# Softmax with one exponential per head, the maximum as bias and the sum accumulated

## The chip, the cores and the metric

One core of a Trainium2 chip. The metric is the device time of one execution in microseconds (us), lower is better. The engines are TensorE (PE; its weight loads are shown apart as PEld), VectorE (DVE), ScalarE (ACT), GpSimd (POOL) and SyncE (SP), which here issues the DMA transfers. Each engine works through a queue of its own in order; they wait for one another by semaphores.

## What is computed

Four graph layers over 128 graphs of 64 nodes with 512 features, all in float32, each with a residual and a layer normalization: a hypergraph convolution, a layer whose weights are exp(tanh) of pair sums, three graph convolutions, and attention with 8 heads of 64 features. The change is in the softmax of the last layer. Cut to what matters:

```python
qkv = (x @ W_qkv).reshape(B, N, HEADS, 3, DIM_HEAD)
q, k, v = (jnp.transpose(qkv[..., i, :], (0, 2, 1, 3)) for i in range(3))
dots = jnp.einsum('bhid,bhjd->bhij', q, k) * scale
dots = jnp.where(m2, dots, -big)
attn = jax.nn.softmax(dots, axis=-1) * LA
attn = attn + LG * adj + LD * jnp.exp(-dist)
out = jnp.einsum('bhij,bhjd->bhid', attn, v)
...
x = _layernorm(x + (out @ W_out + b_out), axis=-1)
```

## The kernel before

The 128 graphs are worked on in 16 groups (NGRP) of 8 graphs, that is 4 pairs of 128 rows. Every group goes through a first half (layers 0 and 1, `first_half`, L753) and a second half (layers 2 and 3, `second_half`, L1079). Three groups are in flight: while group q is in its softmax and output (called t in the list), group q + 1 is in the second half (b), and group q + 2 in the first half (a). The order is written out by hand as lists of step names (L1440 and on): `t.v1 a.c1 t.v b.gt t.soft a.w1a1 a.w1a t.soft2 ... t.ptp`. Inside such an order a scheduler places the instructions on each engine, except where `strict` or `behind` holds them.

All large products go through `multiply` (L546), a scheme with seven products of half size for eight: B11, T1, T2, B21, T3, B22, T4, each of four matmuls, on two or three PSUM banks. Between the products partial results have to be read out of a bank before the next product may add to it:

- after B11 into bank a: `u1`, a copy (L555); T2 adds into bank a afterwards
- after T1 into bank c: `u5` (L555); B22 adds into it later
- after T2 into bank a: `u2` (L555); T3 adds into bank a afterwards
- after T3 into bank a: the addition `dst(1, 1) = pa + s5` (L589); T4 adds into bank a afterwards
- at the end two more additions (L568 for B21, L598 for B22) and a copy of T4's bank (L608)

For the product v of the softmax's own group the copies L555 and L608 are ScalarE's, and the additions L568, L589 and L598 are VectorE's. For the product l0w (the first layer of group q + 2) the read-outs L555 are VectorE's, since a bias is added with them.

The operands of these products are prepared by `graph_T` (L470): matmuls into `gt_l` in PSUM, copied by ScalarE (L492) into `aT_l`, from which VectorE makes the sums `s_l` (`sums`, L518 to L521). The rectifications of l0w's result `h` are ScalarE's (L783).

The softmax of a group works on four tiles (two duos of pairs, two halves h2 of the heads) of 128 rows by 8 heads by 64 columns. `scores` (L1345) takes the products out of PSUM with scale and mask (L1367). `softmax_steps` (L1330) does for each tile: the maximum per head (L1334, VectorE), the subtraction (L1336, VectorE), one exponential over all 512 columns (L1337, ScalarE), the sum per head (L1340, VectorE), its reciprocal (L1341) and the product with it (L1342). The first two tiles are done beside v, the third at `t.soft`, the fourth at `t.soft2`; then `turn_probs` (L1382) turns the tiles on TensorE (`ptp`). ScalarE keeps one table of functions at a time; the first exponential of a group stands behind a table load.

Of the kernel before, what the change touches and what calls it, by code (L numbers as in the profile page):

```python
# [10 lines left out]
AF = mybir.ActivationFunctionType  # L11
ALU = mybir.AluOpType
AX = mybir.AxisListType
# [28 lines left out]
def kernel(  # L42
# [31 lines left out]
    NGRP = NPAIR // G  # L74
# [56 lines left out]
    ten, vec, act = Engine(nc.tensor, PE), Engine(nc.vector, DVE), Engine(nc.scalar, ACT)  # L131
# [305 lines left out]
    def bcast(t, n):  # L437

        return t.unsqueeze(2).to_broadcast([P, n, C])
# [806 lines left out]
    def last_rows(g, probs, v, left):  # L1246
# [4 lines left out]
        next(gen)  # L1251
        yield "v1"
        steps = [[softmax_steps(g, duo, probs[duo], h2) for h2 in range(2)] for duo in range(2)]
        for n in range(2):
            for h2 in range(2):
# [74 lines left out]
    def softmax_steps(g, duo, ds, h2):  # L1330

        d, key = ds[h2], f"{g['q']}_{duo}_{h2}"
        mx = small.tile([P, 8], FP, name=f"mx_{key}", tag="mx")
        vec.reduce_max(mx, d, axis=AX.X)  # L1334
        yield
        vec.tensor_sub(d, d, bcast(mx, 8))  # L1336
        act.activation(d, d, AF.Exp)  # L1337
        yield
        sm = small.tile([P, 8], FP, name=f"sum_{key}", tag="sum")
        vec.reduce_sum(sm, d, axis=AX.X)  # L1340
        vec.reciprocal(sm, sm)  # L1341
        vec.tensor_mul(d, d, bcast(sm, 8))  # L1342
        yield
# [34 lines left out]
    def softmax(g, duo, ds, h2s):  # L1378
        for h2 in h2s:
            whole(softmax_steps(g, duo, ds, h2))  # L1380
# [230 lines left out]
```

## Time and profile before

| what | value |
|---|---|
| time of the runs | 2734.22 us median of 3 (2732.8, 2734.22, 2735.39) |
| profiled execution: its span | 2732.1 us (what lies around the span is not listed apart) |
| TensorE busy | 2714.7 us, 99% |
| weight loads of TensorE busy | 2347.7 us, 86% |
| VectorE busy | 2077.8 us, 76% |
| ScalarE busy | 803.9 us, 29% |
| maximum, subtraction, sum, product of the softmax (L1334, L1336, L1340, L1342) | 676, 686, 681, 690 ns each, 60 of each and 4 more in the last group under another line |
| exponential over 512 columns (L1337) | 628 ns each, 64 |
| table load of ScalarE | 1283 ns each |
| granted clock of TensorE | 1.00 |

How to read it: busy time of an engine is the time in which it executes; a pair "mean 628" beside "x64" is the duration of one instruction from its start to its written result, and instructions that follow each other overlap, so the pitch from start to start is shorter. In the timeline each row has a start, the time that the row covers, the engine, the line of the kernel, the operation with its result and operands, and in brackets how long the engine sat idle before it and whose result ended that. In rows of groups the numbers behind the bar are the busy time in all, the mean of one in ns, and the engine's idle time before them.

### The profile page before, as it was taken

The page shows a single profiled execution, that of the slowest core. Times are in us where ns is not written, and L with a number is a line of the kernel's source. Part 1 is how long each engine was busy: PE and PEld are TensorE (multiplying, and loading weights), DVE is VectorE, ACT ScalarE, POOL GpSimd, SP SyncE. Part 2 cuts the span into 40 slices and gives each one's busy share as a digit, 9 for nine tenths or more (in the row PEclk, how much of TensorE's full clock was granted, in tenths as well). Part 3 has the DMA queues.
Part 4 walks back from the last instruction along what each step waited for, and adds up shares of the span by engine and source line. Part 5 has one row for each costly group of instructions (what it writes and reads, how often), then busy time and mean ns, then how long its engine had stood idle before and what let it go on. Part 6 is the DMA issues. An engine that isn't in the chain of part 4 may idle for free.

```text
span 2732.1 us, 67726 instructions
## 1 busy us (share of the span) xinstructions
PE 2714.7 (99%) x28770; PEld 2347.7 (86%) x28770; DVE 2077.8 (76%) x4111; ACT 803.9 (29%) x1440; POOL 38.0 (1%) x71
## 2 busy tenths in 40 slices
PE   9999999999999999999999999999999999999998
PEld 7888888888888888888888888888888888888887
DVE  6878687876877778777786877778677687776766
ACT  3323223232232332323223233232322323233232
POOL 2000000000000000000000000000000000000000
PEclk9999999999999999999999999999999999999999
DMA  7545454454544545455454554545545455454541
GB/s 257 179 129 154 123 175 140 142 162 131 173 131 139 168 129 170 130 145 168 134 165 129 146 165 133 164 129 151 163 130 167 130 154 157 128 166 129 158 125 63
DMA packets 309532, 405.14 MB, mean 148 GB/s; under 512 B 57424, under 2 KB 185456, under 8 KB 309232
## 3 DMA queue, kind: packets, MB, share of 16 engines
q1 hardware_dynamic: 304256, 385.45, 48.2%
q0 software_dynamic: 4832, 15.24, 1.5%
q8 instruction: 228, 3.74, 0.6%
q14 instruction: 72, 0.59, 0.1%
q10 hardware_dynamic: 144, 0.13, 0.0%
HBM read 369.78 MB, written 30.93 MB: 147 GB/s over the span
## 4 chain that ended last, share of the span: by engine, by line
PE 96%; DVE 3%; ACT 1%; issue 0%; DMA 0%; DVEq 0%
PE a_l0w L539 15%; PE b_l0w L539 7%; PE a_l2b L539 4%; PE a_q L539 4%; PE a_k L539 4%; PE a_l2a L539 4%; PE a_v L539 4%; PE c_l0w L539 4%; PE a_l1w L539 4%; PE a_wo L539 4%; PE a_l2c L539 4%; PE gt_l L481 3%; PE gt_l0h L481 2%; PE b_l2a L539 2%; PE b_l1w L539 2%; PE b_l2b L539 2%
## 5 line engine op out<-in xcount | busy, mean ns | idle before, releaser
L539 PE MATMUL a_l0w<-w2w,aT_l0h 128*128 128x256 f32 x720 | 164.3, 381 | 0.0
L457 DVE BATCH_NORM_STATS2 st_l<-x 128x6 f32<-128x512 f32 x244 | 157.9, 676 | 0.6
L539 PEld LDWEIGHTS a_l0w<-w2w,aT_l0h 128*128 128x128 f32 x720 | 135.6, 190 | 18.8
L463 DVE TENSOR_SCALAR x<-x,mv_l,rs_l 128x512 f32<-128x512 f32 x244 | 119.3, 543 | 2.2
L539 PE MATMUL b_l0w<-w2w,s_l0h 128*128 128x256 f32 x480 | 108.5, 379 | 0.0
L783 ACT ACTIVATE h<-h 128x1024 f32<-128x1024 f32 (+1 forms) x58 | 55.0, 948 | 178.5 <-DVE h L598 157.4
L539 PEld LDWEIGHTS b_l0w<-w2w,s_l0h 128*128 128x128 f32 x480 | 91.1, 190 | 12.5
L1140 ACT ACTIVATE aT_h<-gth,gb_col 128x256 f32<-128x256 f32 x124 | 47.2, 491 | 159.0 <-PE gth L1128 159.0
L447 ACT ACTIVATE rs_l<-mv_l,eps_t 128x4 f32<-128x4 f32 (+1 forms) x63 | 18.8, 298 | 252.3 <-DVE mv_l L458 245.0
L492 ACT COPY aT_l<-gt_l 128x512 f32<-128x512 f32 x148 | 78.1, 597 | 46.4 <-PE gt_l L481 46.4
L555 DVE TENSOR_TENSOR u_l0w<-a_l0w,b_bc 128x512 f32<-128x512 f32 x56 | 38.6, 689 | 69.2 <-PE a_l0w L539 69.2
L539 PE MATMUL a_l2b<-gwbw,aT_h 128*128 128x256 f32 x360 | 86.6, 383 | 0.0
L539 PE MATMUL a_l2c<-gwcw,aT_h 128*128 128x256 f32 x360 | 86.3, 382 | 0.0
L539 PE MATMUL a_q<-aT_xT,wqw 128*128 128x256 f32 x360 | 85.1, 379 | 0.5 <-ACT aT_xT L1194 0.5
L539 PE MATMUL a_l1w<-ww,aT_l 128*128 128x256 f32 x360 | 85.1, 379 | 0.2 <-ACT aT_l L492 0.2
L539 PE MATMUL a_l2a<-aT_l,gwaw 128*128 128x256 f32 x360 | 85.0, 379 | 0.0
L539 PE MATMUL a_k<-aT_xT,wkw 128*128 128x256 f32 x360 | 85.0, 379 | 0.0
L539 PE MATMUL a_v<-wvw,aT_xT 128*128 128x256 f32 x336 | 81.1, 384 | 0.5 <-issue 0.5
L539 PE MATMUL a_l0w<-w1aw,aT_l 128*128 128x256 f32 x336 | 80.8, 383 | 0.0
L539 PE MATMUL a_wo<-wow,aT_oT 128*128 128x256 f32 x336 | 79.5, 379 | 0.0
L539 PE MATMUL a_l0w<-w1bw,aT_l 128*128 128x256 f32 x336 | 79.4, 379 | 0.0
L539 PEld LDWEIGHTS a_l2c<-gwcw,aT_h 128*128 128x128 f32 x360 | 67.2, 190 | 11.6 <-ACT u_l2c L555 3.0
(532 smaller groups left out, 6489.0 us busy)
## 6 DMA issues: line engine op xcount, KB each, us to landing
w2w<-w2k SPq DMA_DIRECT2D x210, 256.0 KB, 2.7
x<-in_x_dram SPq DMA_DIRECT2D x15, 1024.0 KB, 5.8
w1aw<-w1ak SPq DMA_DIRECT2D x60, 256.0 KB, 2.7
w1bw<-w1bk SPq DMA_DIRECT2D x60, 256.0 KB, 2.8
ww<-wk SPq DMA_DIRECT2D x60, 256.0 KB, 2.7
gwaw<-gwak SPq DMA_DIRECT2D x60, 256.0 KB, 3.4
gwbw<-gwbk SPq DMA_DIRECT2D x60, 256.0 KB, 2.7
gwcw<-gwck SPq DMA_DIRECT2D x60, 256.0 KB, 2.7
```

Of the source, the lines that this page charges most:

```text
L447: act.activation(rs[:, at], mv[:, at, 1], AF.Sqrt, bias=eps_t)
L457: vec.bn_stats(st, xg[:, p, :])
L463: vec.tensor_scalar(xg[:, p, :], xg[:, p, :], mv[:, p, 0:1], rs[:, p : p + 1], ALU.subtract, ALU.mult)
L481: ten.matmul(ps[g][f * C : (f + 1) * C, c, p, :], src(2 * duo + p)[rows, c0 : c0 + C], mat[rows, 2 * duo + p, :], start=True, stop=True,)
L492: act.copy(o[:, :, :, g, :], ps[g])
L539: ten.matmul(acc[:, blk, :], lhsT, rhs, start=(first and blk == 0 and i == 0), stop=(last and i == n_k - 1), skip_group_check=True,)
L555: last_add[f"{key}.{what}"] = (act.copy(t, ps) if res is None else vec.tensor_add(t, ps, res(m, n))).ins
L783: act.activation(hn, hn, AF.Relu)
L1140: act.activation(o[:, :, h, :], cols, AF.Relu, bias=gb2_col[:, k : k + 1])
```

## The change

For the groups 1 to 14 (`by_heads`) the maximum is taken with its sign turned, and the exponential is issued once per head: 8 instructions of 64 columns, each with the head's negated maximum as bias column and the sum over the 64 columns as accumulated output. The subtraction and the sum on VectorE fall away there. Groups 0 and 15 keep the old instructions. The points at which the steps can be interrupted (`yield`) stay where they were: behind the maximum, and behind the exponential; they are used for group 15 alone.

```diff
         mx = small.tile([P, 8], FP, name=f"mx_{key}", tag="mx")
-        vec.reduce_max(mx, d, axis=AX.X)
-        yield
-        vec.tensor_sub(d, d, bcast(mx, 8))
-        act.activation(d, d, AF.Exp)
+        by_heads = 0 < g["q"] < NGRP - 1
+        if by_heads:
+            vec.tensor_reduce(mx, d, axis=AX.X, op=ALU.max, negate=True)
+        else:
+            vec.reduce_max(mx, d, axis=AX.X)
         yield
         sm = small.tile([P, 8], FP, name=f"sum_{key}", tag="sum")
-        vec.reduce_sum(sm, d, axis=AX.X)
+        if by_heads:
+            for n in range(8):
+                act.activation(d[:, n], d[:, n], AF.Exp, bias=mx[:, n : n + 1], accum_out=sm[:, n : n + 1])
+        else:
+            vec.tensor_sub(d, d, bcast(mx, 8))
+            act.activation(d, d, AF.Exp)
+        yield
+        if not by_heads:
+            vec.reduce_sum(sm, d, axis=AX.X)
         vec.reciprocal(sm, sm)
         vec.tensor_mul(d, d, bcast(sm, 8))
         yield
```

## The prediction

> **What bounds the kernel now.** I read the page's totals and chain first, then the groups by shape, then one steady stretch of the timeline (908 to 975 us). All times below are from the profiled execution.
>
> ```profile
> PE 2714.7 (99%) x28770; PEld 2347.7 (86%) x28770; DVE 2077.8 (76%) x4111; ACT 803.9 (29%) x1440; POOL 38.0 (1%) x71
> ...
> PE 96%; DVE 3%; ACT 1%; issue 0%; DMA 0%; DVEq 0%
> ```
>
> TensorE works without a gap: 2714.7 of 2732.1 us busy, and it is 96% of the chain that ends last. VectorE time taken away is worth nothing by itself; all that can be had is the 17.4 us in which TensorE isn't busy, 5.3 of them one wait at the start. A delay of TensorE, however, lengthens the run by its whole length. So I ask where ScalarE and VectorE hand something to TensorE with little to spare. The stretch of one softmax:
>
> ```profile
> 915.16 1.27 DVE L1334 TENSOR_REDUCE mx<-sm 128x8 f32<-128x512 f32 x2
> ...
> 916.84 0.59 ACT L555 COPY u_v<-a_v 128x512 f32<-128x512 f32 x1 [3.87 <-PE a_v L539]
> 917.45 1.28 ACT L1337 ACT_TABLE_LOAD   x1
> ...
> 918.10 1.70 PEld L539 LDWEIGHTS a_v<-wvw,s_xT 128*128 128x128 f32 x8
> ...
> 918.74 0.63 ACT L1337 ACTIVATE sm<-sm 128x512 f32<-128x512 f32 x1
> 919.28 0.57 ACT L555 COPY u_v<-b_v 128x512 f32<-128x512 f32 x1
> ...
> 921.35 2.05 ACT L492 COPY aT_l<-gt_l 128x512 f32<-128x512 f32 x4 [0.46 <-PE gt_l L481]
> ...
> 923.43 0.69 DVE L518 TENSOR_TENSOR s_l<-aT_l 128x512 f32<-128x512 f32 x1 [0.82 <-ACT aT_l L492]
> ...
> 925.50 1.70 PEld L539 LDWEIGHTS b_v<-wvw,s_xT 128*128 128x128 f32 x8
> ...
> 926.57 0.68 DVE L589 TENSOR_TENSOR v<-a_v,u_v 128x512 f32<-128x512 f32 x1
> 927.31 1.62 PEld L539 LDWEIGHTS a_v<-wvw,aT_xT 128*128 128x128 f32 x8
> ```
>
> The last two lines matter most. T4, the last product of v, adds into the bank that L589 has to read first. L589 ends at 926.57 + 0.68 = 927.25 and T4's weights start at 927.31. Products come 1.73 apart (916.37, 918.10), so 925.50 + 1.73 = 927.23 was its turn: it has already waited 0.08 us. VectorE has no slack here at all. Similarly T2 (918.10) needs the copy that ended at 917.43, 0.67 us earlier.
>
> **What the change removes and adds.** In 14 of 16 groups (q = 1 to 14) each of four tiles loses a subtraction (0.686) and a sum (0.681) on VectorE: 56 x 1.37 = 77 us of VectorE work, nearly all beside TensorE work, so worth nothing. The maximum keeps its price (negated in the same instruction). On ScalarE one exponential per tile becomes eight; the old one advances the queue by 919.28 - 918.74 = 0.54.
>
> **The price of one head.** Rows of small ScalarE instructions with a column as bias, and VectorE's read of an accumulator:
>
> ```profile
> L1105 ACT ACTIVATE aT_h<-aT_h,gb_col 128x512 f32<-128x512 f32 x56 | 37.4, 715 | 74.2 <-DVE aT_h L598 73.7
> ...
> L447 ACT ACTIVATE rs_h<-mvh,eps_t 128x2 f32<-128x2 f32 x30 | 7.2, 288 | 0.2
> ```
>
> ```profile
> L829 DVE DVE_READ_ACCUMULATOR xwa<-x,wa_bc 128x1 f32 x60 | 5.1, 85 | 0.0
> ```
>
> In the timeline two of the first take 1.33 together, so the pitch is 1.33 - 0.715 = 0.62; two of the second take 0.48, so the pitch is 0.48 - 0.288 = 0.19. Slope: 0.43 / 510 = 0.84 ns a column. For 64 columns: pitch 0.19 + 62 x 0.00084 = 0.24, duration 0.34. An accumulated output on VectorE shows as an instruction of its own; on ScalarE the trace has none. Its ends: nothing (the four VectorE pairs at 851 us keep the pitch of 0.61 without a read), and a read that nothing overlaps, 0.34 + 0.30 = 0.64 a head. I take 0.15: VectorE's read is about half its smallest computation (85 against 162 ns for the 128x2 reciprocal), and half of 288 ns is 0.15. So a head costs e = 0.39, between 0.24 and 0.64. ScalarE gains 448 x 0.39 - 56 x 0.54 = 145 us in all and would still be only a third busy, but the heads fall where it is needed.
>
> **The walk through one group** (e = 0.39, clock times of the old trace). In the changed kernel's instruction order ScalarE has: table load, 2 heads, u_v, 4 heads, u_v, 4 heads, u_v, 5 heads, two copies of gt_l, 1 head, two copies. The load now stands behind a wait for the first maximum (915.16 + 0.67, so 915.9).
> - T2: load to 917.2, two heads to 918.0, copy to 918.56; T2 starts at 918.61 instead of 918.10: **0.51**.
> - T4: 4 heads and a copy (918.5 to 920.56), 4 heads (922.12), the third copy (922.65), 5 heads (924.60), two gt_l copies at 0.49 (925.58), the 16th head, two copies: the last starts at 926.46 and ends at 927.05. VectorE stands in its queue order at the reciprocals of both sums, and behind them are s_l (L518 to L521) and only then the v additions, L568 and L589. Its second reciprocal starts at 926.1; the sums need the last copy, so L518 starts at 927.10 instead of 923.43. Four operations (0.71 + 3 x 0.61) and L568 (0.61) later L589 starts at 930.25 and ends at 930.93. T4 starts at 930.98; its turn would be 927.23 + 0.51 = 927.74. Wait 3.24, less the old 0.08: **3.16**. The 2.4 us of VectorE work saved here doesn't help: it is spent waiting for ScalarE.
> - Third tile: its maximum (behind L598, 930.86) ends at 932.15; 2 heads, the copy of v (T4's result, 933.0), 5 heads, two copies, the last head, done 936.97. Behind its reciprocal and product stands u_l0w (L555), now 937.87, done 938.55. The next T2 would come at 934.63 + 3.67 = 938.30: **0.30**.
> - Fourth tile: 8 heads stand between the two rectifications (L783). With TensorE 3.97 late, the first ends its turn at 947.6, heads to 950.74, second to 951.72, copy u_l2a to 952.31. T2 of l2a, for which half of the product c_l2a is moved ahead in the new order, would come at 951.55: **0.81**. T3 then has only that other half in front of it: 0.18.
>
> Sum 4.96. Group 14 does its third and fourth tiles together; there T2 of l2a waits for 16 heads, and with the first two waits it loses about 5.0. In total 14 x 4.95 = 69 us: the span goes from 2732.1 to 2801. The runs' median is 2.1 above the span (2734.22), so **2803**. Elsewhere queues are unchanged, and DMA (SP, POOL) keeps its order.
>
> One cost more is possible. TensorE idled 5.28 us at the start, and the first 128 gt_l matmuls behind that took 3.79 us where such a set takes 2.10 later; the granted clock is 1.00 in both stretches, so the clock row doesn't show why. If a long wait brought that back each time, 14 x (3.79 - 2.10) = 24 us would come on top; I leave it out of the sum, since my longest wait, 3.24, is shorter than that one, and keep it for the upper end. [...]
>
> **Rivals.**
> - *A cheap read* (e 0.24 to 0.34). The same walk at 0.24 gives T2 0.22, T4 1.1, T3 0.18: 1.5 a group, 21 us, **2755**; at 0.34, 3.4 a group, 2782. For it: VectorE's read takes no pitch at all.
> - *A read that drains ScalarE* (0.46 to 0.64). At 0.64: T2 1.0, T3 of v 0.5, T4 6.2, u_l0w 2.2, l2a 3.0: 12.9 a group, 181 us, **2915**, plus some of the 24 us for restarts. For it: the sum must be complete before it can be read.
> - *Not slower.* VectorE, rid of four operations before L589, comes earlier, and T4's wait of 0.08 us goes: 14 x 0.08 = 1 us, **2733**. It decides where the first 16 heads and 7 copies let L518 start by 923.4, that is with e below about 0.12; the pitch of 0.24 without any read speaks against it. Even every idle us of TensorE in these stretches gains only a few us.
>
> **How the numbers follow.** Forecast (e 0.34 to 0.46, 2782 to 2832) 0.48; cheap read 0.27; draining read 0.20; not slower 0.04; something between that and the cheap read 0.01. The range takes in both ends of e and a few restarts: 2757 to 2920. A measurement here can tell about 0.2% (5.5 us) from no change. Faster 0.01, same 0.03, slower 0.96.
>
> **What would show it.** In the new profile: waits of TensorE (weights of a_v) for VectorE of about 3 us, 14 times, with VectorE in turn waiting for ScalarE before the second reciprocal and L518; a row of accumulator reads on ScalarE and the pitch of a head; ScalarE near a third busy and VectorE near 73%. If the head's pitch is 0.24, 2755 to 2760 follows. I am wrong in mechanism, not size, if TensorE's waits before T4 stay below 0.5 us or if the time is lost outside these 14 stretches.

## The result, and the profile after

The changed kernel takes 2774.59 us (median of 4 runs, 2773.4 to 2778.61) against 2734.77 us for the kernel before (4 runs beside them, 2732.8 to 2735.39): 1.0152 times as long, 95% interval 1.0139 to 1.0164. The profiled execution took 2775.11 us, its span 2773.3, 41.2 more than before. I had predicted slower, with 2803 in a range of 2757 to 2920: the sign and the place were right, the size was 69 us for 40. Of the experiments below, one execution of run 5 took 7638 us and one of run 9 took 5726 us; the medians leave both out, and run 9 has no other trace.

The totals and the chain of work that ended last, in the profile after:

```profile
span 2773.3 us, 68454 instructions
...
PE 2729.6 (98%) x28770; PEld 2346.4 (85%) x28770; DVE 2003.8 (72%) x3999; ACT 915.4 (33%) x2280; POOL 37.9 (1%) x71
...
PE 88%; DVE 7%; ACT 5%; issue 1%; DMA 0%; DVEq 0%; ACTq 0%
```

VectorE has 74 us less work and the kernel is slower: VectorE and ScalarE, 4% of the chain before, are now 12% of it. TensorE, idle for 17.4 us before, is idle for 43.7. The groups say what ScalarE does per head and who waits for it (behind the bar: busy time, mean ns of one, idle time ahead of it and its releaser):

```profile
L1343 ACT ACTIVATE sm<-sm,mx 128x64 f32<-128x64 f32 x448 | 150.7, 340 | 71.2 <-DVE mx L1336 71.1
...
L1350 DVE RECIPROCAL sum<-sum 128x8 f32<-128x8 f32 x60 | 12.0, 201 | 156.5 <-ACT sm L1343 156.4
...
L1343 ACT ACTIVATION_READ_ACCUMULATOR sm<-sm,mx 128x1 f32 x448 | 85.7, 191 | 0.0
```

The read of the accumulator is an instruction of its own, 191 ns long. And VectorE stands for 156 us at the reciprocals, waiting for the heads. The waits of TensorE's weight loads (total, number, longest):

```profile
PEld a_v L539 <- DVE v L589: 30.6, 14, 2.4
...
PEld a_l2a L539 <- ACT u_l2a L555: 7.7, 27, 0.3
...
PEld a_v L539 <- ACT u_v L555: 5.4, 12, 0.7
```

So T4 of v waits for L589 in all 14 groups; this is the large one. One group of the timeline shows the chain behind it. Here ScalarE, from the load to the copies of gt_l, and VectorE and TensorE's weights of v:

```profile
925.10 1.28 ACT L1343 ACT_TABLE_LOAD   x1 [2.94 <-DVE mx L1336]
...
926.39 0.35 ACT L1343 ACTIVATE sm<-sm,mx 128x64 f32<-128x64 f32 x1
926.65 0.19 ACT L1343 ACTIVATION_READ_ACCUMULATOR sm<-sm,mx 128x1 f32 x1
926.74 0.33 ACT L1343 ACTIVATE sm<-sm,mx 128x64 f32<-128x64 f32 x1
...
927.69 1.59 PEld L539 LDWEIGHTS a_v<-wvw,s_xT 128*128 128x128 f32 x8 [0.43 <-ACT u_v L555]
...
930.15 0.20 DVE L1350 RECIPROCAL sum<-sum 128x8 f32<-128x8 f32 x1 [3.34 <-ACT sm L1343]
...
934.10 1.06 ACT L492 COPY aT_l<-gt_l 128x512 f32<-128x512 f32 x2
934.24 0.20 DVE L1350 RECIPROCAL sum<-sum 128x8 f32<-128x8 f32 x1 [3.16 <-ACT sm L1343]
934.48 0.69 DVE L1351 TENSOR_TENSOR sm<-sm,sum 128x512 f32<-128x512 f32 x1
...
935.19 0.69 DVE L518 TENSOR_TENSOR s_l<-aT_l 128x512 f32<-128x512 f32 x1
...
938.33 0.68 DVE L589 TENSOR_TENSOR v<-a_v,u_v 128x512 f32<-128x512 f32 x1
938.93 0.68 DVE L598 TENSOR_TENSOR v<-b_v,u_v 128x512 f32<-128x512 f32 x1
939.06 1.77 PEld L539 LDWEIGHTS a_v<-wvw,aT_xT 128*128 128x128 f32 x8 [2.38 <-DVE v L589]
```

Two heads start at 926.39 and 926.74: with its read a head advances the queue by 0.33 to 0.35 us, though the exponential lasts 0.35 and the read 0.19; the two overlap. VectorE idles 3.34 and 3.16 us in front of the reciprocals, and only then come the four sums and L568, which need nothing of the softmax, and L589. L589 ends at 939.01, and T4 starts at 939.06.

The sums need one thing more, the last copy of gt_l, which stands behind the heads in ScalarE's queue. It ends at 934.10 + 1.06 = 935.16, and L518 starts at 935.19. From T2's start to that end are 7.47 us; before it was 923.40 - 918.10 = 5.30. The difference, 2.17, is all that T4 loses. The second tile's product on VectorE ends at 935.17, so this trace alone doesn't tell which of the two queues decides; run 2 does.

From the starts of the weight loads I get one group's loss. The time between successive L589 of v is 167.97 us before and 170.81 after in most groups: 2.84 a group. T1 to T2 takes 2.13 or 2.14 instead of 1.73 (+0.41); T2 to T4 11.37 or 11.38 instead of 9.21 (+2.17); T4 to T2 of l0w 7.29 instead of 7.32; what is left to 2.84 (+0.29) lies in l2a. Two of the 14 groups lost 1.55 and 1.69 us more behind T4 (at a granted clock of 0.50; the last section shows where), and in three groups T4 waited only 1.2 to 1.7 us.

### The profile page after: what moved, and what is told of

Same layout as the page of the kernel before. It is cut to its first block, busy times and chain, and to the rows that moved or that the text cites. A ratio compares the mean times of both kernels' runs of the same rounds, so it can differ in the third digit from the quotient of the medians.

```text
span 2773.3 us, 68454 instructions
## 1 busy us (share of the span) xinstructions
PE 2729.6 (98%) x28770; PEld 2346.4 (85%) x28770; DVE 2003.8 (72%) x3999; ACT 915.4 (33%) x2280; POOL 37.9 (1%) x71
## 4 chain that ended last, share of the span: by engine, by line
PE 88%; DVE 7%; ACT 5%; issue 1%; DMA 0%; DVEq 0%; ACTq 0%
PE a_l0w L539 15%; PE b_l0w L539 7%; PE a_l2a L539 4%; PE a_l2b L539 4%; PE a_q L539 4%; PE a_k L539 4%; PE c_l0w L539 4%; PE a_l1w L539 4%; PE a_wo L539 4%; PE a_l2c L539 4%; ACT sm L1343 3%; PE gt_l L481 2%; PE gt_l0h L481 2%; PE b_l2a L539 2%; PE b_l1w L539 2%; PE b_l2b L539 2%
## 5 line engine op out<-in xcount | busy, mean ns | idle before, releaser
L1343 ACT ACTIVATE sm<-sm,mx 128x64 f32<-128x64 f32 x448 | 150.7, 340 | 71.2 <-DVE mx L1336 71.1
L1350 DVE RECIPROCAL sum<-sum 128x8 f32<-128x8 f32 x60 | 12.0, 201 | 156.5 <-ACT sm L1343 156.4
L539 PEld LDWEIGHTS a_v<-wvw,aT_xT 128*128 128x128 f32 x336 | 62.7, 193 | 40.4 <-DVE v L589 30.6
L1343 ACT ACTIVATION_READ_ACCUMULATOR sm<-sm,mx 128x1 f32 x448 | 85.7, 191 | 0.0
```

What stands on the lines that cost most here:

```text
L539: ten.matmul(acc[:, blk, :], lhsT, rhs, start=(first and blk == 0 and i == 0), stop=(last and i == n_k - 1), skip_group_check=True,)
L1343: act.activation(d[:, n], d[:, n], AF.Exp, bias=mx[:, n : n + 1], accum_out=sm[:, n : n + 1])
```

## The experiments

The main theory, "queue": the loss is the order of the queues. The heads delay the copies of gt_l on ScalarE and the reciprocals on VectorE, the sums and L589 stand behind both, and T4 waits. (The expectations below name VectorE's queue; which queue decides is told at run 2.) The main rival, "load": ScalarE's 118 us of added work (448 x 0.33 less 56 x 0.54) cost about a third of themselves wherever they stand, as contention would. Each kernel was timed beside the kernel before, whose medians were 2733.7 to 2734.4 us. "Per group" is always the time between successive L589 of v, less the 167.97 us of before.

**1. The read taken away.** Heads with bias but without accumulated output; the sum is VectorE's again.

```diff
-                act.activation(d[:, n], d[:, n], AF.Exp, bias=mx[:, n : n + 1], accum_out=sm[:, n : n + 1])
+                act.activation(d[:, n], d[:, n], AF.Exp, bias=mx[:, n : n + 1])
...
-        if not by_heads:
-            vec.reduce_sum(sm, d, axis=AX.X)
+        vec.reduce_sum(sm, d, axis=AX.X)
```

> The heads keep their bias but lose the accumulated output; VectorE takes the sum of each tile again (56 x 0.68 = 38 us more VectorE work than in the changed kernel), the subtraction stays away. Theory (queue): the loss comes because the first 16 heads and the copies among them hold VectorE's queue, and with it L518 to L521 and L589, beyond the turn of T4. Without the read a head should advance ScalarE by 0.24 instead of 0.33 us, the wait before T4 shrinks from 2.38 to about 1.0 us, and about 1.5 us a group is lost: 14 x 1.5 = 21 us, 2755 us, although VectorE works 38 us more. Rival (load): the loss goes with the work added to ScalarE wherever it falls, 40 us for 448 x 0.33 - 56 x 0.54 = 118 us, 0.34 us per us; here 448 x 0.24 - 30 = 78 us are added, so 26 us, 2761 us. Rival (VectorE's work counts): the sums put back cost again, 2774 us or more.

Measured 2751.32 us (ratio 1.0064, 1.0047 to 1.0081), 1.34 us per group; T4 waits 0.84. In ScalarE's timeline six heads in a row, then a copy:

```profile
922.47 1.54 ACT L1343 ACTIVATE sm<-sm,mx 128x64 f32<-128x64 f32 x6
923.91 0.57 ACT L555 COPY u_v<-a_v 128x512 f32<-128x512 f32 x1
```

Six heads take 923.91 - 922.47 = 1.44, so 0.24 each: the slope of the prediction was right, and the read costs 0.33 - 0.24 = 0.09. With 39 us more work on VectorE (2042.7 against 2003.8) the kernel is 23 us faster: work on VectorE is not what the change pays with. Against "load" (2761) it speaks by 10 us, less sharply than the next ones.

**2. A dearer head.** A column of ones as scale.

```diff
-..., AF.Exp, bias=mx[:, n : n + 1], accum_out=sm[:, n : n + 1])
+..., AF.Exp, bias=mx[:, n : n + 1], scale=ones[:, 0:1], accum_out=sm[:, n : n + 1])
```

> The heads keep bias and accumulated output and get a column of ones as scale too: the same values, one more operand read from a column. If that column makes a head dearer (say from 0.33 to 0.42 us), the theory (queue) says the loss rises steeper than the work: by the walk 5.8 us a group, 81 us, 2815 us, with waits before T4 of 4 us or more and more of the 3.4 us stretches at half the granted clock (2 of 14 groups in the changed kernel). Rival (load): 448 x 0.42 - 30 = 158 us added to ScalarE at 0.34 us per us is 54 us, 2788 us. If the head's pitch stays at 0.33, both say 2775 us and nothing is learnt.

Measured 2812.06 us (1.0288, 1.0272 to 1.0303). ScalarE's timeline:

```profile
935.69 0.43 ACT L1343 ACTIVATE sm<-sm,mx,ones 128x64 f32<-128x64 f32 x1
936.02 0.19 ACT L1343 ACTIVATION_READ_ACCUMULATOR sm<-sm,mx,ones 128x1 f32 x1
936.12 0.43 ACT L1343 ACTIVATE sm<-sm,mx,ones 128x64 f32<-128x64 f32 x1
```

The pitch is 0.43. Another 0.09 us a head, 40 us of work on ScalarE, cost 37 us of time, where "load" gave 14: the loss is steep, as a queue's is. But my list of waits was wrong: T4 waits 3.13 and not 4. In this order three heads of the second tile stand behind the first two copies of gt_l and one behind all four; the delay that this spares T4 comes back at l0w (13.9 us in 13 waits for u_l0w). And the granted clock, 0.50 in stretches of 3.41 us, took a part: 5.10 us in groups without a drop (71 us in all), up to 6.8 in those with one.

This order also tells the two queues apart. VectorE's timeline:

```profile
942.03 0.69 DVE L518 TENSOR_TENSOR s_l<-aT_l 128x512 f32<-128x512 f32 x1 [4.43 <-ACT aT_l L492]
...
945.04 0.68 DVE L589 TENSOR_TENSOR v<-a_v,u_v 128x512 f32<-128x512 f32 x1
945.65 0.19 DVE L1350 RECIPROCAL sum<-sum 128x8 f32<-128x8 f32 x1
```

The second reciprocal stands behind L589 here, and T4 waits all the same: L518 idles 4.43 us for the last copy of gt_l. So the late copies in ScalarE's queue are enough to hold T4. In all traces but run 9's, before and after the change, L518 starts 0.03 us behind that copy in each of the groups 0 to 14.

**3 and 4. Half of the heads.** First in the two tiles ahead of T4 alone, then in the other two alone.

```diff
-        by_heads = 0 < g["q"] < NGRP - 1
+        by_heads = 0 < g["q"] < NGRP - 1 and duo == 0
```

> Heads only in the first two tiles of a group (those in front of T4); the third and fourth tile have the old subtraction, whole exponential and sum. Theory (queue): the waits before T2 and T4 stay as in the changed kernel (about 2.4 before T4, 0.4 before T2), only l2a's 0.3 goes: 2.5 us a group, 35 us, 2769 us. Rival (load): half of the heads, half of the loss, 20 us, 2754 us.

> Heads only in the third and fourth tile of a group, none in front of T4. Theory (queue): T4 waits 0.1 us as in the kernel before, what is left are l2a's waits of 0.3 us: about 0.35 us a group, 5 us, 2739 us. Rival (load): half of the loss, 20 us, 2754 us.

(The second has `duo == 1`.) Measured 2769.14 us (1.0129, 1.0114 to 1.0144), 2.55 per group, and 2738.88 us (1.0019, 1.0009 to 1.0028), 0.34 per group. The same 224 heads on ScalarE cost 35 us in one place and 5 in the other, together the 40 of the change. "Load" (2754 for both) is out.

**5. The first two tiles moved back**, one behind the second product of v, one behind all of v.

```diff
-        softmax(g, 0, probs[0], (0, 1))
+        with behind(f"v_{q}.u1"):
+            softmax(g, 0, probs[0], (0,))
         with behind(f"v_{q}"):
+            softmax(g, 0, probs[0], (1,))
             softmax(g, 1, probs[1], (0,))
```

> All heads and reads are kept; only places change: the first tile's exponentials and products come behind the second product of v, the second tile's with the third's behind the whole of v. So ScalarE's 16 heads and VectorE's reciprocals that wait for them no longer all stand in front of L518 and L589. Theory (queue): most of the 2.4 us before T4 goes, 0.5 to 1 us may be left for the first tile, and the second and third tile's reciprocals now stand in front of the l0w copies: 1.0 to 1.7 us a group in all, 2749 to 2758 us. Rival (load): ScalarE has the same 118 us more, so 2775 us as in the changed kernel.

Measured 2760.88 us (1.0099, 1.0084 to 1.0114), 1.90 per group: better by 14 us with the same work, but above my 2749 to 2758. TensorE's weights in one group:

```profile
931.82 1.59 PEld L539 LDWEIGHTS a_v<-wvw,aT_xT 128*128 128x128 f32 x8 [1.08 <-DVE v L589]
...
943.22 1.59 PEld L539 LDWEIGHTS a_l0w<-w1aw,aT_l 128*128 128x128 f32 x8 [0.68 <-DVE u_l0w L555]
...
946.94 1.59 PEld L539 LDWEIGHTS a_l0w<-w1aw,aT_l 128*128 128x128 f32 x8 [0.41 <-DVE h L589]
```

T4's part fell from 2.17 to 0.97 us a group, since eight heads and not 16 stand ahead of the copies of gt_l. But 0.82 us came back at l0w: the reciprocals of two tiles now stand ahead of its read-outs.

**6. The saving alone.** Groups 1 to 14 keep the whole-tile exponential and leave out the subtraction of the maximum and the sum; the product goes with the reciprocal of the maximum.

```diff
-        by_heads = 0 < g["q"] < NGRP - 1
+        by_heads = False
...
-            vec.tensor_sub(d, d, bcast(mx, 8))
+            if g["q"] in (0, NGRP - 1):
+                vec.tensor_sub(d, d, bcast(mx, 8))
             act.activation(d, d, AF.Exp)
...
-        if not by_heads:
+        if g["q"] in (0, NGRP - 1):
             vec.reduce_sum(sm, d, axis=AX.X)
-        vec.reciprocal(sm, sm)
+            vec.reciprocal(sm, sm)
+        else:
+            vec.reciprocal(sm, mx)
```

> The change's saving without its cost: groups 1 to 14 take the whole-tile exponential of the kernel before, but leave out the subtraction of the maximum and the sum (the product goes with the reciprocal of the maximum), 56 x 1.37 = 77 us less VectorE work than before and nothing more on ScalarE. Theory (queue): VectorE's time is worth nothing but the old 0.08 us before T4: 2732 to 2734 us. Rival (VectorE is a second bound, its saving worth a part and the heads costing the more): 0.2% or more below before, 2728 us or less.

Measured 2743.23 us (1.0032, 1.002 to 1.0044): neither. With 75 us less VectorE work and not one instruction more on ScalarE it is slower by 0.68 us a group. The timeline shows why:

```profile
918.08 1.28 ACT L1347 ACT_TABLE_LOAD   x1 [2.95 <-DVE mx L1338]
...
919.37 1.15 ACT L1347 ACTIVATE sm<-sm 128x512 f32<-128x512 f32 x2
...
920.43 0.57 ACT L555 COPY u_v<-a_v 128x512 f32<-128x512 f32 x1
```

Rid of the subtraction, the exponentials are ready earlier, and the scheduler puts the table load and both of them ahead of the first copy u_v, for which T2 waits (0.81 us). This is the wait of the prediction's T2 term by itself. Saving work on one engine made another engine's queue worse.

**7. The same saving, with the order of before**: on top of run 6's edit, the first two tiles' exponentials behind the second product of v.

```diff
-        softmax(g, 0, probs[0], (0, 1))
+        with behind(f"v_{q}.u1"):
+            softmax(g, 0, probs[0], (0, 1))
```

> As in the run without subtraction and sum (groups 1 to 14 leave out both, the product goes with the reciprocal of the maximum; whole-tile exponentials), but the first two tiles' exponentials are issued behind the second product of v, so that the table load stands behind the first copy u_v again, as in the kernel before. Theory (queue): the 0.68 us a group that the run without this order lost was T2's wait for that copy (0.81 us before its weights), which is gone: 2731 to 2735 us, no gain from 77 us less VectorE work. Rival (VectorE's time does matter, and the loss hid it): 2728 us or less. Second rival (the loss lay elsewhere): 2743 us again.

Measured 2733.45 us (0.9999, 0.999 to 1.0008), 0.00 per group. VectorE's 74 us (2003.7 against 2077.8 us busy) are worth nothing that can be measured.

**8. All the work kept, both queues cleared further.** The reciprocal and product of the first tile come behind the second product of v, those of the second and third behind l0w, the heads of these two behind v. The sums s_l are given out one step later, so that they may stand among the additions of v.

```diff
+        yield "c1"
         left.sums()
-        yield "c1"
...
-        softmax(g, 0, probs[0], (0, 1))
+        steps = [[softmax_steps(g, duo, probs[duo], h2) for h2 in range(2)] for duo in range(2)]
+        with behind(f"v_{q}.u1"):
+            whole(steps[0][0])
         with behind(f"v_{q}"):
-            softmax(g, 1, probs[1], (0,))
+            for late in (steps[0][1], steps[1][0]):
+                for n in range(2):
+                    next(late)
...
-            softmax(g, 1, probs[1], (1,))
+            whole(steps[0][1])
+            whole(steps[1][0])
+            whole(steps[1][1])
```

> All heads, reads and copies are kept, 448 x 0.33 us on ScalarE as in the changed kernel, but VectorE's queue meets no reciprocal of a tile that isn't ready: the first tile's come behind the second product of v, those of the second and third tile behind l0w, with the heads of both behind v. Theory (queue): the wait before T4 falls to 0.3 us or less, what is left is the wait of l2a for u_l2a behind the last 8 heads, about 0.3 us, and the copies of gt_l behind the heads: 0.3 to 0.7 us a group, 2738 to 2744 us. Rival (load): 2775 us as in the changed kernel. A third reading (the copies u_v and u_l0w on ScalarE and VectorE are late behind any heads, wherever put): 2755 us or more.

Measured 2754.89 us (1.0075, 1.0063 to 1.0088): above the expectation, but with 0.74 us per group. The rest is at another place, a wait at the start, in group 1's first layer, that the moved sums made:

```profile
90.93 3.06 PEld L127 LDWEIGHTS b_l0w<-w1aw,s_l 128*128 128x128 f32 x8 [5.85 <-DVE s_l L127]
```

In the steady groups VectorE's queue and T4 stand like this:

```profile
932.27 0.20 DVE L1356 RECIPROCAL sum<-sum 128x8 f32<-128x8 f32 x1 [5.46 <-ACT sm L1349]
932.51 0.69 DVE L1357 TENSOR_TENSOR sm<-sm,sum 128x512 f32<-128x512 f32 x1
934.19 0.69 DVE L518 TENSOR_TENSOR s_l<-aT_l 128x512 f32<-128x512 f32 x1 [0.98 <-ACT aT_l L492]
...
936.72 0.69 DVE L589 TENSOR_TENSOR v<-a_v,u_v 128x512 f32<-128x512 f32 x1
```

There is one reciprocal ahead of L589 and no second one, and the wait of 5.46 us for it ends while there is still time. What is late, as in the changed kernel, is the last copy of gt_l, now behind eight heads (0.98 us in front of L518). From L518 to L589 are 2.53 us instead of 3.14, since one of the sums (L521) stands behind L589 now. L589 ends 0.37 us after T4's turn (T2 to T4 9.58 instead of 9.21), and T2 is on time (1.73). The heads in front of u_l2a cost 0.39.

**9. The same, with group 1's first layer as it was** (against run 8).

```diff
+        if q == 1:
+            left.sums()
         yield "c1"
-        left.sums()
+        if q > 1:
+            left.sums()
```

> The kernel of the run before with all heads behind (all 448 heads, reads and copies kept, no reciprocal in front of L589 that isn't ready), but with the sums of the very first group's stage left in their old place. There a wait of TensorE for s_l at 91 us took 5.85 us and its next eight weight loads 3.06 instead of 1.59, which the heads have nothing to do with. Theory (queue): that loss of about 7.3 us goes and the 0.74 us a group (168.71 against 167.97 us between groups) stays: 2744 to 2749 us. Rival (load): the rest above before has to do with the heads' work on ScalarE in all, so little goes: 2753 us or more.

Measured 2746.04 us (1.0044, 1.0031 to 1.0058). All 448 heads and reads are there, and of the 40 us of the change 28 are gone by order alone; the third reading of run 8 (2755 or more wherever the heads stand) is out. No kernel here beats the one before, and run 7 says why: there is nothing to be had from VectorE, and a head can at best be hidden.

## Why the prediction was right, and what was mis-sized

- *What bounds the kernel* held: TensorE, with L589 of v the place without slack. VectorE's saving is worth nothing (run 7), T4 pays in every group.
- *The price of a head* was the term that failed in size. The pitch of 0.24 from the slope of two other rows was right (run 1). The read I put at 0.15, half of the smallest computation, and it measured 0.09; its 191 ns overlap the exponentials on both sides. So e is 0.33 and not 0.39, the case I had called the cheap read (0.24 to 0.34, 2755 to 2782; 2774.59 is in it). The time lies in the range, then, but not in the case that I held likeliest (2782 to 2832, 0.48); it is the one I gave 0.27.
- *The walk* held, also in that L518 starts when the last copy of gt_l is there (927.10 in the walk); the traces show this wait in every group (run 2). With 0.06 less a head: T2 of v 0.51 less two heads, 0.39, measured 0.41. T4 3.16 less 16 heads (0.96) and plus the 0.12 by which T2 is less late, 2.3, measured 2.17. l0w's T2 0.30 less eight heads, nothing; measured nothing. l2a 0.81 and 0.18 less eight heads, at most 0.5; measured 0.29. The sum that was 4.96 became 2.84, because 16 heads stand in one row ahead of T4, so that an error of 0.06 us counts 16 times.
- *No mechanism of another kind*: halves of the change add up (35 + 5 = 40), and no time is lost outside these stretches but for the clock's 3 us: 40.5 of the 41.2 us of the span lie between the L589 of group 0 and that of group 14.
- *The rival "not slower"* needed a head below 0.12; even without its read a head takes 0.24, and the kernel was slower by 18 us (run 1). *A read that drains ScalarE* needed 0.46 or more a head and is out at 0.33.
- *Left out of the sum* was a slow stretch behind a wait, since my longest wait was shorter than the one at the start. That reason was wrong: slow stretches, at a granted clock of 0.50, came with waits of 2.38 us, in 2 of 14 groups, 1.55 and 1.69 us each. I had priced one at 1.69. Nor does the 1.00 that I read for the first gt_l set say anything: that set ran from 6.85 to 10.64 us, and the trace's record of the granted clock begins at 11.46.

## What to carry to other kernels

When work moves from an idle engine to another idle engine, ask not what the sum of the work is but which instructions of the path stand behind it in both queues: here copies and sums that need nothing of the softmax stood behind its heads and reciprocals. A saving on an engine that doesn't bound the run can even cost, when it lets a long instruction come ahead of a short urgent one (run 6: 75 us less work on VectorE, 0.68 us a group slower). The price of an unknown small instruction, multiplied by the number that stand in a row before the critical hand-over, is the error of the forecast. Bound the pitch, not the duration: here an exponential of 0.35 us and a read of 0.19 overlapped to a pitch of 0.33.

## What the hardware showed that I had not expected

*The granted clock fell behind waits of 2.38 us, well below the 5.28 us at the start, and not every time.* Each lowered stretch behind a T4 lasted 3.41 us at a granted clock of 0.50, and inside a run their starts lay whole multiples of 3.413 us apart: 425.00 and 940.41 in the changed kernel are 151 such steps apart, 772.35 and 946.43 with the dearer head 51. So I cut the time into these steps. Two groups of the changed kernel, each with the step that holds the wait and the next one (columns: window, its length, busy time and number of TensorE matmuls, of weight loads, VectorE, ScalarE, GpSimd, then the granted clock, DMA share and GB/s):

```profile
937.00:940.41 3.41, 1.43 (x7) 1.22 (x7) 3.20 (x6) 0.17 (x1) 0.00 (x0) 1.00 0.38 130
940.41:943.83 3.42, 3.42 (x92) 2.70 (x94) 0.00 (x0) 2.83 (x16) 0.00 (x0) 0.50 0.23 77
1107.66:1111.07 3.41, 1.78 (x9) 1.22 (x7) 3.38 (x6) 0.00 (x0) 0.00 (x0) 1.00 0.45 142
1111.07:1114.48 3.41, 3.06 (x84) 2.57 (x88) 1.49 (x3) 1.80 (x8) 0.00 (x0) 1.00 0.13 47
```

and of the kernel with the dearer head:

```profile
420.83:424.25 3.42, 1.92 (x9) 1.33 (x8) 2.52 (x5) 1.30 (x4) 0.00 (x0) 1.00 0.60 159
424.25:427.66 3.41, 2.18 (x24) 1.70 (x28) 3.17 (x6) 0.15 (x1) 0.00 (x0) 1.00 0.17 65
943.02:946.43 3.41, 0.68 (x4) 0.60 (x4) 3.38 (x7) 0.00 (x0) 0.00 (x0) 1.00 0.45 127
946.43:949.85 3.42, 3.42 (x43) 2.42 (x45) 1.33 (x3) 0.85 (x3) 0.00 (x0) 0.50 0.03 7
```

Both groups of the first pair waited 2.38 or 2.39 us ahead of T4, and only one lost its clock; both of the second waited 3.13. Counted by the waits of T4's weights in the traces:

| wait ahead of T4 | kernels | with a lowered clock behind it |
|---|---|---|
| 0.84 us | read taken away | 0 of 11 |
| 2.38 to 2.39 us | the change; heads in the first two tiles | 4 of 22 |
| 3.13 to 3.14 us | dearer head | 9 of 11 |

In these traces the groups differ in where the wait falls. TensorE's matmuls paused for 1.98 us in the waits of 2.38. At 937 the whole pause lies in one step (3.41 - 1.43 = 1.98), and the next step has a granted clock of 0.50; at 1107 it lies across a border, and the clock stays at 1.00. Counted over all 33 groups of the last two rows: behind a step with 1.98 us or more without matmuls the clock was lowered (13 groups), behind steps with at most 1.92 it wasn't (20). That is a count and no threshold: run 8 has a drop, at 2636.23, behind a step with 1.86 us without matmuls (the eight weight loads from 2635.55 on took 2.43 us, the eight of that group's T4 1.59). All this is read from traces; no run moved a wait in time.

*The second column had a price of its own.* The scale column of run 2 added 0.09 us to each head (a pitch of 0.42 to 0.43 against 0.33), the same as the read (0.33 against 0.24 in run 1).
